# q and k times their inverse length as one VectorE instruction, and the inverse key sums as 128 rows of 16 columns

## The chip, the cores and the metric

The kernel runs on one core of one Trainium2 chip. The engines are PE (TensorE), DVE (VectorE), ACT (ScalarE) and POOL (GpSimd); SP issues most of the DMAs. The metric is the device time of one launch in microseconds. All arithmetic that the change touches is float32.

## The reference

x has 32 sequences of 256 positions of 256 channels. A recurrent layer (a projection to 512 channels, a causal convolution of four taps, a normalisation, a scan over the 256 positions with 16 states and a gate) gives the input of two attention layers, each followed by a gated feed-forward. x is added to the end result. What the change touches is in the attention layer:

```python
l2norm = lambda t: t / jnp.clip(jnp.linalg.norm(t, axis=-1, keepdims=True), 1e-12)
q, k = l2norm(q) * qs, l2norm(k) * ksc          # 8 heads of 64
q, k = rotary_xpos(q, k)
sim = jnp.where(mask, -max, einsum('bhwid,bhwjd->bhwij', 8 * q, k))   # windows of 128
attn = softmax(sim, axis=-1)
out = einsum('bhwij,bhwjd->bhwid', attn, v)
x = x + out @ wo
```

Two inverses are in it: that of the length of each head's q and k, limited from below, and that of the sum of the exponentials of each query.

## The kernel before

The 32 sequences go in four groups of eight. The scan of a group takes 256 steps, eight sequences at once: at each step SP loads a row of xn, spread over 128 partitions (`load_rows`, L685, six steps ahead), ACT scales it by beta (`scale_row`, L706), DVE takes the step (`step`, L716, one custom instruction of 128x512, whose inputs h and xrep lie in SBUF), and PE reads the states out (`read_out`, L728). Every 32 steps (a chunk) come the convolution of the next chunk (xr L472, acc L478 on POOL and L489 on DVE, xc L509), its normalisation (statistics on DVE, the power -1/2 on POOL in L565, L572 and L579 on ACT), the decays (bcd L632, ad L648, pd L650, pi L653, beta L654), the sum of skip and readout (xd L779) and the gate (zT L799, read by PE in L808).

While group g is scanned, group g-1 goes through attention and feed-forward: 64 pairs of sequence and layer in all. Each pair is a sequence of stages, eight stages (`ST = 8`) to a pair and about two scan steps to a stage; the pairs overlap. `attend` and `feed` (L1458 and L1479) put the functions into numbered stages: `stage(n, i, what)` is stage 8n + i. Two pairs take one chunk of 32 scan steps. The convolution and the decays of a chunk fall into the second of the two, which is called odd here, the other even.

In a pair, for each of two windows w: PE projects v, q and k (`project_qkv`, L989, into PSUM banks of 128x512). For q and k `rotated` (L998) follows: ACT squares (sq, L1002), DVE multiplies by the cosine and sine tables (rot L1005, swp L1010 twice), POOL adds the two (L1013), DVE sums the squares by head (L1015) and limits the sum from below by 1e-24 (L1019), POOL takes the power -1/2 (rn, L1021), and POOL multiplies the rotated tile by it (L1022). `turn` (L1025) transposes the result with PE (L1028), and ACT copies it. Then come the scores on PE (L1215), the exponentials on ACT (L1227) and the masks (L1238 on POOL, L1243 on DVE). `sums` (L1246) adds the exponentials with PE (L1252), into rows of a bank: 16 equal rows for each of the eight heads, 256 columns; DVE takes the reciprocal of all 128x256 (rinv, L1260). `values` (L1263) multiplies with v (L1271), and ACT copies to oT (L1278). `put_inverse` (L1281) stores one of each 16 rows to a tensor in DRAM, `load_inverse` (L1285) reads it back, each head's row spread over 64 partitions (rb), `divide` (L1293) multiplies oT by it on DVE, and `finish` projects (ps_wo, L1039) and adds to the residual (res, L1047). In the feed-forward `widen` (L1361) projects into pa (L1375), ACT applies the Gelu to one half (ag, L1386), DVE multiplies by the other (`product`, L1393), and `narrow` (L1398) projects back (po_f, L1402) and adds (fo or res, L1413).

The PSUM banks are eight and are handed round among all of these, so a projection waits for whoever read the bank's former content. A scheduler orders each engine's instructions at build time, by the order of the program and by when it takes their inputs to be ready; `tc.keep_in_program_order` pins an instruction behind all that its engine was given before. On the chip each engine takes its list strictly in order and waits at an instruction until its inputs are there; so does SP with its DMAs.

Of the kernel before, what the change touches and what calls it, by code (L numbers as in the profile page):

```python
# [10 lines left out]
FP = mybir.dt.float32  # L11
BF = mybir.dt.bfloat16
I32 = mybir.dt.int32
AF = mybir.ActivationFunctionType
ALU = mybir.AluOpType
# [4 lines left out]
P = 128  # L20
S = 256
# [15 lines left out]
HEADS = 8  # L37
DH = 64
W = 128
NW = S // W  # L40
# [12 lines left out]
def bc(ap, axis, n):  # L53

    ap = ap.unsqueeze(axis)
    shape = list(ap.shape)
    shape[axis] = n
    return ap.broadcast_to(shape)
# [15 lines left out]
def kernel(  # L74
# [29 lines left out]
    nc = tc.nc  # L104
# [4 lines left out]
    const = ctx.enter_context(tc.tile_pool(name="const", bufs=1))  # L109
# [14 lines left out]
    with tc.tile_pool(name="setup", bufs=1) as setup:  # L124
        sq = setup.tile([1, L, 2, DH], FP, tag="sq", name="sq")
# [37 lines left out]
    for j in range(NJ):  # L163
# [5 lines left out]
    nc.gpsimd.memset(one, 1.0)  # L169
    neg_half = const.tile([P, HEADS], FP, tag="neg_half", name="neg_half")  # L170
    nc.gpsimd.memset(neg_half, -0.5)
    half = const.tile([P, NJ], FP, tag="half", name="half")
    nc.gpsimd.memset(half, 0.5)

# [7 lines left out]
        out=mask_t[:, 0:W], in_=mask_t[:, 0:W], compare_op=ALU.is_ge, fill=MASKED_LOW,  # L182
# [3 lines left out]
        out=mask_t[:, W : 2 * W], in_=mask_t[:, W : 2 * W], compare_op=ALU.is_ge,  # L186
# [11 lines left out]
    rs_sb = const.tile([P, L, NW, 2, DH], FP, tag="rs_sb", name="rs_sb")  # L198
# [18 lines left out]
    for i in range(2):  # L217
        t = const.tile([P, NI * (P + GB)], FP, tag=f"ly{i}", name=f"ly{i}")
# [3 lines left out]
    def program(ctx, exact):  # L222
# [6 lines left out]
        dp = ctx.enter_context(tc.tile_pool(name="dp", bufs=3, space=DRAM))  # L229
        ap_ = ctx.enter_context(tc.tile_pool(name="at", bufs=2, reuse_waits="tile"))  # L230
        aw = ctx.enter_context(tc.tile_pool(name="aw", bufs=3, reuse_waits="tile"))
        ps_w = ctx.enter_context(tc.tile_pool(name="psw", bufs=8, space=PSUM, reuse_waits="tile"))

        def bank(pool, tag, name):
            return pool.tile([P, DI], FP, tag=tag, name=name)
# [748 lines left out]
        def project_qkv(b, w, a):  # L984
            ps = bank(ps_w, "w", "ps_qkv")
            for k in range(KM):

                t0 = 1 - k + w * W
                nc.tensor.matmul(  # L989
                    ps,  # L990
                    res[b][:, k, t0 : t0 + W],
                    wt["qkv", a][:, k],
                    start=(k == 0),
                    stop=(k == KM - 1),
                )
            return ps

        def rotated(l, ps, w, a):  # L998


            sq = ap_.tile([P, DI], FP, tag="swp", name="sq", bufs=3)
            nc.scalar.activation(sq, ps, AF.Square)  # L1002
            rot = ap_.tile([P, HEADS, DH], FP, tag="rot", name="rot", bufs=4)
            ph = ps.rearrange("p (h d) -> p h d", h=HEADS)
            nc.vector.tensor_mul(rot, ph, bc(rc_sb[:, l, w, a], 1, HEADS))  # L1005
            swp = ap_.tile([P, HEADS, DH], FP, tag="swp", name="swp", bufs=3)
            hd = DH // 2
            for i in range(2):
                o, s = slice(i * hd, (i + 1) * hd), slice((1 - i) * hd, (2 - i) * hd)
                nc.vector.tensor_mul(  # L1010
                    swp[:, :, o], ph[:, :, s], bc(rs_sb[:, l, w, a, o], 1, HEADS)
                )
            nc.gpsimd.tensor_add(rot, rot, swp)  # L1013
            ss = aw.tile([P, HEADS], FP, tag="ss", name="ss")
            nc.vector.tensor_reduce(  # L1015
                ss, sq.rearrange("p (h d) -> p h d", h=HEADS), AX.X, ALU.add
            )

            nc.vector.tensor_scalar_max(ss, ss, 1e-24)  # L1019
            rn = aw.tile([P, HEADS], FP, tag="rn", name="rn")  # L1020
            nc.gpsimd.tensor_tensor(rn, ss, neg_half, ALU.pow)  # L1021
            nc.gpsimd.tensor_mul(rot, rot, bc(rn, 2, DH))  # L1022
            return rot

        def turn(rot, dst):  # L1025
            tr = ps_w.tile([P, HEADS // 2, W], FP, tag="w", name="tr_qk")
            for hp_ in range(HEADS // 2):
                nc.tensor.transpose(  # L1028
                    tr[:, hp_, :],
                    rot[:, 2 * hp_ : 2 * hp_ + 2, :].rearrange("p h d -> p (h d)"),  # L1030
                    ident,
                )
            nc.scalar.copy(dst, tr)
# [15 lines left out]
        if exact:  # L1049
# [4 lines left out]
                out=mask[:, 0:W], in_=mask[:, 0:W], compare_op=ALU.is_ge, fill=MASKED,  # L1054
# [3 lines left out]
                out=mask[:, W : 2 * W], in_=mask[:, W : 2 * W], compare_op=ALU.is_ge, fill=MASKED,  # L1058
# [3 lines left out]
        def attention(l):  # L1062

            for b in range(GB):

                qTs, kTs, vs = [], [], []
                for w in range(NW):
                    for a in (2, 0, 1):
                        ps = project_qkv(b, w, a)
                        if a == 2:  # L1070
                            v_sb = ap_.tile([P, DI], FP, tag="v1", name="v_sb", bufs=3)
                            nc.scalar.copy(v_sb, ps)
                            vs.append(v_sb)
                            continue
                        rot = rotated(l, ps, w, a)
                        dst = ap_.tile(
                            [P, HEADS // 2, W], FP, tag="kT1" if a else "qT1",
                            name="kT" if a else "qT", bufs=3 if a else 2,
                        )
                        turn(rot, dst)  # L1080
                        (kTs if a else qTs).append(dst)
                        yield

                oT = ap_.tile([P, NC_, S], FP, tag="oT", name="oT", bufs=1)
                for w in range(NW):
# [6 lines left out]
                    for h0 in range(0, HEADS // 2, nh):  # L1092
                        for r in range(2):
# [21 lines left out]
                            for i, h in enumerate(hs):  # L1115
                                nc.scalar.activation(
                                    p_sb[:, i, :], p_sb[:, i, :], AF.Exp,
                                    bias=nmax[:, h : h + 1],
# [19 lines left out]
                    rinv = aw.tile([P, HEADS], FP, tag="rinv", name="rinv")  # L1138
# [15 lines left out]
        class Attention:  # L1154
# [9 lines left out]
            def project(self, b, w, a):  # L1164
# [8 lines left out]
                else:  # L1173
                    self.rot[b, w, a] = rotated(self.l, ps, w, a)

            def turn(self, b, w):
                for a in range(2):
                    turn(
                        self.rot.pop((b, w, a)), self.qkv[b][a][:, :, w * W : (w + 1) * W]
                    )  # L1180
# [65 lines left out]
            def sums(self, b):  # L1246

                rs = bank(ps_w, "w", "rs")[:, 0:S]
                for kw in range(NW):
                    for r in range(2):  # L1250
                        for i in range(HEADS // 2):
                            nc.tensor.matmul(  # L1252
                                rs[32 * i : 32 * i + 32, kw * W :],
                                head_cols[:, r],
                                self.p[b, kw, i, r],
                                start=(kw == 0 and r == 0),
                                stop=(kw == NW - 1 and r == 1),
                            )
                rinv = aw.tile([P, S], FP, tag="rinv", name="rinv", bufs=1)
                nc.vector.reciprocal(rinv, rs)  # L1260
                self.rinv = rinv

            def values(self, b):  # L1263
                oT = ap_.tile([P, NC_, S], FP, tag="oT", name="oT", bufs=1)
# [13 lines left out]
                    nc.scalar.copy(oT[:, i0 : i0 + 2], ov)  # L1278
                self.o[b] = oT

            def put_inverse(self):  # L1281
                self.inv = dp.tile([HEADS, S], FP, tag="inv", name="inv")
                nc.sync.dma_start(out=self.inv, in_=self.rinv[0 : P : P // HEADS])

            def load_inverse(self):  # L1285

# [168 lines left out]
        def stage(n, i, what, *args):  # L1455
            stages.setdefault(ST * n + i, []).append(partial(what, *args))

        def attend(n, at, b, nxt):  # L1458

            stage(n, 0, at.turn, b, 1)  # L1460
            stage(n, 2, at.scores, b, (0, 0, 2), (1, 0, HEADS // 2))
            stage(n, 3, at.scores, b, (0, 2, 2))
            stage(n, 3, at.mask, 1, 0)
            if at.apart:
                for i, what in ((3, (0, 0)), (4, (0, 2))):
                    stage(n, i, at.mask, *what)
            stage(n, 7, at.sums, b)
            stage(n, 7, at.values, b)
            stage(n + 1, 0, at.put_inverse)
            stage(n + 1, 2, at.load_inverse)  # L1470
            stage(n + 1, 4, at.divide, b)
            stage(n + 1, 6, at.finish, b)
            if nxt is not None:
                for w in range(NW):
                    for i, a in ((0, 2), (1, 0), (1, 1)):
                        stage(n, 3 * w + i, nxt[0].project, nxt[1], w, a)
                stage(n, 6, nxt[0].turn, nxt[1], 0)

        def feed(n, g, l, b):  # L1479
# [23 lines left out]
        ats = [Attention(g, l) for g, l, _ in seqs]  # L1503

        for n, (g, l, b) in enumerate(seqs):
            nxt = (ats[n + 1], seqs[n + 1][2]) if n + 1 < len(seqs) else None
# [7 lines left out]
        def scan_to(s):  # L1514
            while done[0] is None or done[0] < s:
                done[0] = next(scan, 1 << 30)
# [9 lines left out]
        for w in range(NW):  # L1526
            for a in (2, 0, 1):
                ats[0].project(0, w, a)
                scan_to(done[0] + 1)
        ats[0].turn(0, 0)  # L1530
        s0 = done[0]
        group, reload = ST * L * GB, ST * (L * GB - GB + 6) + 2
# [129 lines left out]
```

## Time and profile before

| | us |
|---|---|
| three runs | 3581.7, 3597.07, 3590.51 (median 3590.51) |
| the profiled execution | 3582.75 |
| its span | 3581.0 |
| mean granted clock of PE | 0.992 of full speed |
| DVE busy in the span's first 500 us / 500 to 2800 / after | 413 / 1852 / 402 |
| PE busy in the same stretches | 446 / 2226 / 773 |

Attention begins at about 475 us; the last scan step starts at 2796 us. A row of groups reads: line, engine, operation, tiles written and read, shapes, count, then busy time in us, mean ns of one, and after the second bar the idle time of the engine ahead of it with what ended it. A row of waits reads: who waited, for whom, us in total, times, longest us. A row of a timeline reads: start, duration, engine, line, operation, tiles, and in brackets the idle time before it and what ended it.

### The profile page before, as it was taken

What the parts mean: (1) busy time and instruction counts of PE and PEld (TensorE: products, weight loads), DVE (VectorE), ACT (ScalarE), POOL (GpSimd) and SP (SyncE); (2) the same over time, 40 slices, a digit from 0 to 9 for tenths busy, and PEclk for the clock granted to TensorE, in tenths of its full rate; (3) what the DMA queues carried; (4) which work ended last, traced back from release to release, by engine and by line L of the source; (5) the groups of instructions that cost most, each with busy time, mean ns of one, the idle gap of its engine ahead of it and who ended that gap; (6) DMA issues with size and microseconds to landing.
All of it is one profiled execution on the core that took longest, in us unless ns stands there. A gap on an engine that the chain in (4) does not pass through costs nothing.

```text
span 3581.0 us, 57673 instructions
## 1 busy us (share of the span) xinstructions
PE 3446.0 (96%) x20220; PEld 2253.9 (63%) x20220; DVE 2667.3 (74%) x5049; ACT 1998.7 (56%) x3599; POOL 1892.2 (53%) x1842
## 2 busy tenths in 40 slices
PE   7999989999999999999999999999999999999999
PEld 4555335666656666666666666666666677777777
DVE  5888889888788777888787778888877555555553
ACT  4666656656555665566566655655666444434442
POOL 4433477645556555655565556555544454544551
PEclk9999999999999999999999999999999999999999
DMA  7887665445354545444454555534454112011101
GB/s 207 219 221 213 198 174 149 120 117 143 109 144 125 149 141 148 130 118 127 118 142 125 138 149 140 143 106 131 114 141 122 54 50 61 13 30 38 33 27 37
DMA packets 468767, 435.68 MB, mean 122 GB/s; under 512 B 228723, under 2 KB 308084, under 8 KB 468340
## 3 DMA queue, kind: packets, MB, share of 16 engines
q1 hardware_dynamic: 384018, 419.88, 42.0%
q10 hardware_dynamic: 84450, 12.01, 2.0%
q8 instruction: 163, 2.67, 0.3%
q14 instruction: 136, 1.11, 0.1%
HBM read 383.54 MB, written 46.66 MB: 120 GB/s over the span
## 4 chain that ended last, share of the span: by engine, by line
PE 61%; DVE 19%; DMA 7%; POOL 6%; ACT 4%; issue 3%; SPq 0%; ACTq 0%; DVEq 0%; POOLq 0%
PE ps_qkv L989 13%; PE pa L1375 13%; DVE h L716 7%; PE po_f L1402 7%; DMA xrep<-xnd 5%; PE ps_wo L1039 5%; PE y L728 4%; PE ov L1271 4%; PE sc L1215 3%; PE ps_out L808 3%; PE ps_in L399 2%; PE tr_qk L1028 2%; PE rs L1252 2%; ACT xrep L706 2%; DVE acc L489 2%
## 5 line engine op out<-in xcount | busy, mean ns | idle before, releaser
L716 DVE CUSTOM_DVE_ANT_0 h<-h,xrep,lim 128x512 f32<-128x512 f32 x1024 | 961.0, 938 | 228.9 <-ACT xrep L706 196.6
L706 ACT ACTIVATE xrep<-xrep,beta 128x512 f32<-128x512 f32 x960 | 672.3, 718 | 341.4 <-DMA xrep<-xnd 219.8
L989 PE MATMUL ps_qkv<-qkv,res 128*128 128x512 f32 x1536 | 713.5, 601 | 17.9 <-DVE rinv L1260 8.4
L1375 PE MATMUL pa<-hT,w 128*128 128x256 f32 (+1 forms) x2816 | 675.1, 382 | 11.3 <-DVE zT L799 10.7
L1375 PEld LDWEIGHTS pa<-hT,w 128*128 128x128 f32 (+1 forms) x2816 | 516.9, 188 | 152.9 <-issue 35.4
L1013 POOL TENSOR_TENSOR rot<-rot,swp 128x512 f32<-128x512 f32 x256 | 339.9, 1328 | 475.3 <-DVE swp L1010 423.5
L1021 POOL TENSOR_TENSOR rn<-ss,neg_half 128x8 f32<-128x8 f32 x256 | 466.8, 1823 | 18.4 <-DVE ss L1019 7.8
L989 PEld LDWEIGHTS ps_qkv<-qkv,res 128*128 128x128 f32 x1536 | 282.2, 191 | 301.6 <-issue 241.4
L728 PE MATMUL y<-h,ly 128*32 128x512 f32 x2048 | 348.9, 609 | 16.9 <-DVE h L716 13.9
L1327 POOL TENSOR_TENSOR rstd<-ve,neg_half 128x2 f32<-128x2 f32 x64 | 46.9, 733 | 527.6 <-DVE ve L1325 511.3
L1393 DVE SCALAR_TENSOR_TENSOR ag<-pa,b_sb,ag 128x256 f32<-128x256 f32 x320 | 151.6, 474 | 222.4 <-ACT ag L1386 222.3
L1402 PE MATMUL po_f<-ag,w 128*128 128x256 f32 x1280 | 309.0, 389 | 5.9 <-DVE fo L1413 3.8
L1022 POOL TENSOR_TENSOR rot<-rot,rn 128x512 f32<-128x512 f32 x256 | 289.4, 1130 | 20.0
L1402 PEld LDWEIGHTS po_f<-ag,w 128*128 128x128 f32 x1280 | 236.8, 191 | 71.3 <-issue 12.0
L1386 ACT ACTIVATE ag<-pa,b_sb 128x256 f32<-128x256 f32 x320 | 150.2, 469 | 233.1 <-PE pa L1375 232.1
L1002 ACT ACTIVATE sq<-ps_qkv 128x512 f32<-128x512 f32 x256 | 150.8, 595 | 185.1 <-PE ps_qkv L989 119.4
L1039 PE MATMUL ps_wo<-oT,wo 128*128 128x256 f32 x1024 | 231.7, 379 | 0.5 <-DVE ag L1393 0.5
L489 DVE SCALAR_TENSOR_TENSOR acc<-xr,wc_sb,acc 128x256 f32<-128x256 f32 x384 | 195.1, 531 | 47.7 <-POOL acc L478 47.2
L1005 DVE TENSOR_TENSOR rot<-ps_qkv,rc_sb 128x512 f32<-128x512 f32 x256 | 174.8, 683 | 65.6 <-ACT sq L1002 65.0
L1039 PEld LDWEIGHTS ps_wo<-oT,wo 128*128 128x128 f32 x1024 | 194.4, 190 | 28.1 <-DVE ag L1393 0.9
L1227 ACT ACTIVATE pT<-sc 128x512 f32<-128x512 f32 x384 | 202.3, 603 | 7.6 <-PE sc L1215 5.8
L1271 PE MATMUL ov<-pT,v_sb 128*64 128x256 f32 (+1 forms) x2048 | 183.7, 330 | 19.4 <-DVE ag L1393 19.3
(160 smaller groups left out, 5482.8 us busy)
## 6 DMA issues: line engine op xcount, KB each, us to landing
xrep<-xnd SPq DMA_DIRECT2D x960, 256.0 KB
rb<-inv SPq DMA_DIRECT2D x128, 256.0 KB
xnd<-xn SPq DMA_DIRECT2D x64, 256.0 KB
qkv<-in_wqkv_dram SPq DMA_DIRECT2D x24, 512.0 KB
ahead<-xs_a SPq DMA_DIRECT2D x48, 256.0 KB
xp<-ahead SPq DMA_DIRECT2D x48, 256.0 KB
xd<-xnd SPq DMA_DIRECT2D x192, 64.0 KB
w<-in_w_dram SPq DMA_DIRECT2D x80, 128.0 KB
```

What stands on the lines that cost most here:

```text
L489: nc.vector.scalar_tensor_tensor(acc, xr[:, :, k : k + CH], wc_sb[:, ch, k : k + 1], acc, ALU.mult, ALU.add,)
L706: scaled = nc.scalar.activation(bx, ck[c].pop(("bx", t), bx), AF.Copy, scale=ck[c]["beta"][:, t : t + 1])
L716: nc.vector._custom_dve(TENSOR_ADD_SAT, out=h_new, in0=state["h"], in1=bx, s0=ck[c]["lim"][:, 0, t : t + 1], s1=ck[c]["lim"][:, 1, t : t + 1],
L728: nc.tensor.matmul(ck[c]["y", hb][32 * q : 32 * q + 32, :], ly[hb % 2][:, 32 * t : 32 * t + 32], ck[c].pop(("h", hb * TB + t)), start=(i = ...
L989: nc.tensor.matmul(ps, res[b][:, k, t0 : t0 + W], wt["qkv", a][:, k], start=(k == 0), stop=(k == KM - 1),)
L1013: nc.gpsimd.tensor_add(rot, rot, swp)
L1021: nc.gpsimd.tensor_tensor(rn, ss, neg_half, ALU.pow)
L1022: nc.gpsimd.tensor_mul(rot, rot, bc(rn, 2, DH))
L1039: nc.tensor.matmul(po[:, d], wt["wo", 0][:, c, d * P : (d + 1) * P], oT[:, c, :], start=(c == 0), stop=(c == NC_ - 1),)
L1271: nc.tensor.matmul(ov[r * DH : (r + 1) * DH, i, kw * W :], self.qkv[b][2][:, kw, h * DH : (h + 1) * DH], self.p.pop((b, kw, i0 + i, r)), s ...
L1375: nc.tensor.matmul(dst[x], wt["w1", m][:, k, x], self.h[:, k], start=(k == 0), stop=(k == KM - 1),)
L1402: nc.tensor.matmul(self.po[:, d], wt["w2", 0][:, m, d * P : (d + 1) * P], self.ag[m], start=(m == 0), stop=(m == len(MCH) - 1),)
```

## The change

The limit and the product with the inverse length become one scalar_tensor_tensor on DVE, min(rn, 1e12) times rot, in a function `unit` of its own. It is pinned, and `normed` puts it two stages after the projection of q and k. The squares get a bias of 2e-19 (tile `tiny`) ahead of squaring. The sums of the exponentials are copied from PSUM by ACT, one of each 16 rows is stored to DRAM, read back as 128 rows of 16 columns, inverted there by DVE (pinned), stored to DRAM, and read back spread as before. The divide moves from stage 4 to stage 5.

```diff
+    tiny = const.tile([P, 1], FP, tag="tiny", name="tiny")
+    nc.gpsimd.memset(tiny, 2e-19)
...
-            nc.scalar.activation(sq, ps, AF.Square)
+            nc.scalar.activation(sq, ps, AF.Square, bias=tiny)
...
-
-            nc.vector.tensor_scalar_max(ss, ss, 1e-24)
             rn = aw.tile([P, HEADS], FP, tag="rn", name="rn")
             nc.gpsimd.tensor_tensor(rn, ss, neg_half, ALU.pow)
-            nc.gpsimd.tensor_mul(rot, rot, bc(rn, 2, DH))
+            return rot, rn
+
+        def unit(rot, rn):
+
+            tc.keep_in_program_order(
+                nc.vector.scalar_tensor_tensor(
+                    rot, bc(rn, 2, DH), 1e12, rot, ALU.min, ALU.mult
+                )
+            )
             return rot
...
+            def normed(self, b, w):
+                for a in range(2):
+                    self.rot[b, w, a] = unit(*self.rot[b, w, a])
...
-                rinv = aw.tile([P, S], FP, tag="rinv", name="rinv", bufs=1)
-                nc.vector.reciprocal(rinv, rs)
-                self.rinv = rinv
+                self.rs = aw.tile([P, S], FP, tag="rinv", name="rs_sb", bufs=1)
+                nc.scalar.copy(self.rs, rs)
...
+            def put_sums(self):
+                self.sm = dp.tile([HEADS, S], FP, tag="sums", name="sums")
+                nc.sync.dma_start(out=self.sm, in_=self.rs[0 : P : P // HEADS])
+
+            def load_sums(self):
+                self.r16 = aw.tile([P, HEADS * S // P], FP, tag="r16", name="r16", bufs=1)
+                nc.sync.dma_start(
+                    out=self.r16,
+                    in_=self.sm.rearrange("h (q t) -> (h q) t", q=P // HEADS),
+                )
+
+            def invert(self):
+                tc.keep_in_program_order(nc.vector.reciprocal(self.r16, self.r16))
+
             def put_inverse(self):
                 self.inv = dp.tile([HEADS, S], FP, tag="inv", name="inv")
-                nc.sync.dma_start(out=self.inv, in_=self.rinv[0 : P : P // HEADS])
+                nc.sync.dma_start(
+                    out=self.inv.rearrange("h (q t) -> (h q) t", q=P // HEADS), in_=self.r16
+                )
...
-            stage(n + 1, 0, at.put_inverse)
-            stage(n + 1, 2, at.load_inverse)
-            stage(n + 1, 4, at.divide, b)
+            stage(n + 1, 0, at.put_sums)
+            stage(n + 1, 1, at.load_sums)
+            stage(n + 1, 2, at.invert)
+            stage(n + 1, 2, at.put_inverse)
+            stage(n + 1, 3, at.load_inverse)
+            stage(n + 1, 5, at.divide, b)
             stage(n + 1, 6, at.finish, b)
             if nxt is not None:
                 for w in range(NW):
                     for i, a in ((0, 2), (1, 0), (1, 1)):
                         stage(n, 3 * w + i, nxt[0].project, nxt[1], w, a)
+                    stage(n, 3 * w + 3, nxt[0].normed, nxt[1], w)
                 stage(n, 6, nxt[0].turn, nxt[1], 0)
...
+        for w in range(NW):
+            ats[0].normed(0, w)
         ats[0].turn(0, 0)
```

The path for large scales (not taken with these inputs) calls `unit(*rotated(...))` at once.

## The prediction

> **What bounds the kernel now.** First the page's busy times, then the waits of PE between 500 and 2800 us (there the scan and the attention of another group run side by side), then the timelines of PE and DVE over one period.
>
> ```profile
> PE 3446.0 (96%) x20220; PEld 2253.9 (63%) x20220; DVE 2667.3 (74%) x5049; ACT 1998.7 (56%) x3599; POOL 1892.2 (53%) x1842
> PE 61%; DVE 19%; DMA 7%; POOL 6%; ACT 4%; issue 3%; SPq 0%; ACTq 0%; DVEq 0%; POOLq 0%
> ```
>
> PE is busy for 96% of the span and leads the chain that ended last. The change touches no matmul, so it can only win where PE stands still. Who makes it stand still, in total us, times and longest:
>
> ```profile
> PE ov L1271 <- DVE ag L1393: 19.3, 14, 1.5
> PE pa L1375 <- DVE zT L799: 10.7, 8, 1.9
> PE ps_qkv L989 <- DVE rinv L1260: 8.4, 14, 0.9
> ...
> PE ps_qkv L989 <- DVE xd L779: 2.6, 9, 0.5
> ```
>
> These four, 41.0 us or 1.1% of the span, are all waits for DVE, and they come back in every period of 32 scan steps (103 us, two sequences of attention). From 2800 us on PE waits for DVE 0.6 us in all; before 500 us its waits are for loads and the scan. One period, from the start of one wait to the end of the third:
>
> ```profile
> 1977.39 1.99 PE L1375 MATMUL pa<-hT,w 128*128 128x256 f32 x8 [1.16 <-DVE zT L799]
> ...
> 1983.64 1.52 PE L1271 MATMUL ov<-pT,v_sb 128*64 128x256 f32 x16 [1.37 <-DVE ag L1393]
> ...
> 1990.16 1.98 PE L989 MATMUL ps_qkv<-qkv,res 128*128 128x512 f32 x4 [0.78 <-DVE rinv L1260]
> ```
>
> ```profile
> 1975.73 1.01 DVE L1019 TENSOR_SCALAR ss<-ss 128x8 f32<-128x8 f32 x1
> 1976.66 0.68 DVE L799 TENSOR_TENSOR zT<-tz,sg 128x512 f32<-128x512 f32 x1
> ...
> 1980.16 1.02 DVE L648 TENSOR_SCALAR ad<-ad,a_sb 128x32 f32<-128x32 f32 x1
> 1981.10 1.83 DVE L716 CUSTOM_DVE_ANT_0 h<-h,xrep,lim 128x512 f32<-128x512 f32 x1
> ...
> 1983.04 0.45 DVE L1393 SCALAR_TENSOR_TENSOR ag<-pa,b_sb,ag 128x256 f32<-128x256 f32 x1
> ...
> 1988.36 1.75 DVE L1260 RECIPROCAL rinv<-rs 128x256 f32<-128x256 f32 x1
> ```
>
> DVE has no idle time from 1962.9 to 1986.2 us: in this odd sequence of the period it is late, and PE waits three times. A limit over 8 columns (L1019) takes 1.01 us right ahead of zT, though the fastest of its kind takes 0.15; POOL was running its product L1022 then (1975.55, 1.17 us). The ad of 32 columns, 1.02 us, ran beside the next L1022 (1980.08, 1.07 us). In the even sequence (1990 to 2043 us) DVE has idle times of 2.84 and 5.79 us, and PE waits only 0.52 us, for xd.
>
> **The change, part by part.** Rows (count, busy us, mean ns):
>
> ```profile
> L716 DVE CUSTOM_DVE_ANT_0 h<-h,xrep,lim 128x512 f32<-128x512 f32 x1024 | 961.0, 938 | 228.9 <-ACT xrep L706 196.6 <-DVE h L716 8.7 <-PE y L728 2.3
> L1022 POOL TENSOR_TENSOR rot<-rot,rn 128x512 f32<-128x512 f32 x256 | 289.4, 1130 | 20.0
> L1019 DVE TENSOR_SCALAR ss<-ss 128x8 f32<-128x8 f32 x256 | 119.8, 468 | 0.6
> L1260 DVE RECIPROCAL rinv<-rs 128x256 f32<-128x256 f32 x64 | 112.0, 1750 | 11.1 <-PE rs L1252 10.6 <-DMA rw<-raw 0.5
> L1295 DVE TENSOR_TENSOR oT<-oT,rb 128x1024 f32<-128x1024 f32 x64 | 77.6, 1213 | 0.0
> ```
>
> POOL loses 256 products, 289.4 us. POOL is not the bound, but its next work comes 2.2 us earlier per pair of q and k (two products).
>
> DVE loses 256 limits (119.8 us) and 64 wide reciprocals (112.0 us). It gains 256 products of 128x512 with two inputs from SBUF. No row has this form. A scalar_tensor_tensor of 256 columns takes 478 ns (L1413); from 256 to 512 columns L1010 (415) and L1005 (683) grow by 268; so 0.75 us, 192 us in all. The ends are half of L1295, 0.61 (156 us), and the scan step L716 with its two SBUF inputs, 0.94 (241 us). The narrow reciprocal: 1750 ns at 256 columns, 341 at 32 (L653), so 6.3 ns a column and 0.24 us at 16, 15 us in all. DVE's sum is 192 + 15 - 120 - 112 = -25 us (-61 to +24). As a total that matters little; its place does.
>
> ACT gains 64 copies of 128x256 from PSUM, between 0.36 (64x256, L526) and 0.58 (128x512, L1278); I take 0.45, 29 us, beside PE. It stands ahead of the copies of oT and delays them by that; ps_wo, which needs them, runs some 35 us later. The bias of the square adds no instruction.
>
> SP gets two more small DMAs per sequence. One put and the wait for its landing took 1.72 us (inv issued at 1990.14, rb behind it at 1991.86). So the sums go out behind the copy at about 1988.5, are back after two trips at 1992.0, and the built order has the reciprocal just ahead of the next q (before: 1998.8): 6.8 us of cover. Behind it on DVE wait the q and k work and the scan steps, should this cover go. On SP the put of the inverse now waits for that DVE reciprocal; the loads of xrep behind it need a later scan step anyway. The divide stands one stage later and, by the even sequence's times (done at 2019.8, ps_wo at 2023.4), still 3.6 us ahead of ps_wo.
>
> Now the odd sequence by the built order. (1) Two products (1.5 us) come in front of the convolution, at 1956.3. There DVE waited 0.47, 0.30 and 0.64 us for POOL's acc (L478), which comes 2.2 us sooner: net +0.1; the reordered block behind it (xc, acc, xr, divide) keeps its sum, and some 0.9 us of small gaps and long xc go; DVE reaches q about 1.0 us sooner at best, 0 at worst. (2) Two L1019 go, 0.34 and 1.01 us: zT is 1.3 to 2.3 us sooner, and PE's 1.16 us **goes**. (3) Then ag: res (0.67 us) and two products (1.5) now stand ahead of it; against that the 1.3 to 2.3 won, and up to 1.0 each in ad and in the h of 1.83 us. So ag comes about 1 us earlier than before, and PE, no longer held at zT, arrives 1.16 earlier: this wait **stays**. (4) rs leaves PSUM by the ACT copy at about 1988.3 instead of 1990.1: PE's 0.78 **goes**, and the bank's next user is not late. (5) In the even sequence L1019 (0.33 + 0.16) leaves the queue ahead of xd and 0.24 enters: 0.3 of 0.5 us of that wait goes.
>
> Sum over the span: zT 10.7 + rinv 8.4 + xd 1.6 = **20.7 us** less. The profiled execution took 3582.75 us (span 3581.0), which gives 3562. The median of the runs shown is 3590.51, 7.8 above it; a median of new runs is then 3569.8, my number.
>
> A rule against this change: the row h L716 takes 0.81 us in its median, 0.94 in its mean, and 1.83 beside POOL's xd (1981.11, 1.27 us). [...]
>
> **Rivals.**
> A, the product runs at 0.94 us because POOL is at work beside it: four of them ahead of ag, 4 x 0.19 = 0.76 us later in each of 22 periods, 17 us: the gain shrinks to 4 us, 3586. For: h's mean. Against: part of h's excess came from the L1022 that goes.
> B, ag's wait goes too, since ad and h lose their POOL neighbour and (1) gives its full 1.0 us: 41 us less, 3549. Against: POOL's xd still stands there.
> C, slower: the even sequence becomes like the odd one. The divide (1.2 us) leaves DVE's idle time at 2015 us and stands behind ag at 2018.5, ahead of q and k; with the two products behind them (1.5) DVE is up to 2.7 us later where PE now never waits. It decides if PE's slack there is under that. If PE loses 2 us in each of 22 even sequences, the sum is +44 - 21 = +23, 3614. Against: zT was done at 2023.5 and first used at 2027.7, 4.2 us of slack, and the idle time of 5.79 us behind takes up the products. For: PSUM banks freed by ag and q have a slack that no row shows.
> D, the narrow inverse lands late and holds DVE. It needs 6.8 us more than the row; I give it little. From 0 at that point each us costs up to 64.
>
> **How the numbers follow.** Forecast 0.44, A 0.28, B 0.10, C 0.14, D 0.04. About 0.5% (18 us) is what a measurement here can tell from no change, so faster means under 3572.6. The forecast lies just beyond: a sixth of its 0.44 falls within. Faster 0.37 + 0.10 and a little of A: 0.50; slower C and D less 0.03 that stays within, 0.15; the same 0.35. The range takes in B (less 10 for PE waits on h and fo that also shrink) and the product's upper end with half of C: 3539 to 3601.
>
> **What would show it.** Right: no PE wait on rinv's successor and none on zT, ag still the first of PE's waits; product at 0.7 to 0.8 us; ad's median (1015 ns) lower; DVE some 25 us less, POOL 289 less; DVE never waiting at the narrow reciprocal. Wrong: products near 1 us, a new PE wait between 2005 and 2043 us of the like period, or DVE idle in front of the reciprocal.

## The result and the profile after

The changed kernel takes 3546.99 us (median of 4 runs, 3541.36 to 3553.66), the kernel before 3589.3 (4 runs, 3581.7 to 3597.07). The ratio is 0.9883, 95% interval 0.9865 to 0.9902: 42 us faster. The forecast was 21. The profiled execution took 3553.66 us, with a span of 3551.9.

First the page's busy times and the shares of the chain that ended last, in the changed kernel:

```profile
PE 3441.7 (97%) x20220; PEld 2263.7 (64%) x20220; DVE 2605.5 (73%) x5049; ACT 2037.4 (57%) x3663; POOL 1620.7 (46%) x1587
PE 64%; DVE 16%; DMA 7%; ACT 5%; POOL 4%; issue 3%; SPq 1%; ACTq 0%; DVEq 0%; POOLq 0%
```

PE's work is the same, its share grew, and DVE's share of the chain fell from 19 to 16%. DVE lost 62 us of busy time, POOL 272, and ACT gained 39. Where PE stood still is best seen in the stretches 1000 to 2500 us, here their sum lines, before and after:

```profile
sum 1500.00, PE 1453.63 PEld 963.51 DVE 1205.73 ACT 899.74 POOL 878.06; mean PE 484.54 PEld 321.17 DVE 401.91 ACT 299.91 POOL 292.69
```

```profile
sum 1500.00, PE 1480.16 PEld 982.25 DVE 1190.16 ACT 937.99 POOL 773.47; mean PE 493.39 PEld 327.42 DVE 396.72 ACT 312.66 POOL 257.82
```

PE's idle time there went from 46.4 to 19.8 us. This number (1500 less PE's busy time) is used below for every kernel. One period of 32 scan steps took 102.3 us before and 99.6 after (mean over steps 448 to 896, by the starts of h). The stretch from the last scan step to the end is 785.2 us before and 785.3 after. From the first scan step to the last it is 2748.3 and 2707.4 us, 40.8 less; the two spans differ by 29.1 only since in this one execution the scan began 11.7 us later (at 59.2): the granted clock was 0.63 from 20 to 40 us and 0.67 from 40 to 60, against 1.00 and 0.83 before. Of the 40.8 us, 24.6 are idle time of PE; the other 16.2 stand in the profile as shorter busy time of the same matmuls, whose ends are modelled. An estimate from the granted clock (0.997 against 0.989 over 586 us of PE work in steps 448 to 640) puts some 5 of them down to it; the rest is open.

Who makes PE wait between 500 and 2800 us, in the changed kernel (total us, times, longest):

```profile
PE ps_wo L1047 <- DVE oT L1322: 11.2, 4, 6.1
PE ps_qkv L991 <- DVE ag L1420: 7.2, 12, 1.4
...
PE pa L1402 <- DVE zT L801: 5.1, 7, 0.7
PE ps_qkv L991 <- DVE xd L781: 4.5, 13, 0.4
```

The wait of ov on ag, 19.3 us and first of all before, is not in the list any more. That of ps_qkv on the reciprocal (8.4) is gone too, zT's is halved (10.7), xd's grew (2.6). The odd sequence that the prediction walked through, on PE and then on DVE:

```profile
1961.11 2.00 PE L1402 MATMUL pa<-hT,w 128*128 128x256 f32 x8 [0.68 <-DVE zT L801]
...
1964.47 2.82 PE L1282 MATMUL ov<-pT,v_sb 128*64 128x256 f32 x32
```

```profile
1955.59 0.68 DVE L1007 TENSOR_TENSOR rot<-ps_qkv,rc_sb 128x512 f32<-128x512 f32 x1
...
1960.37 0.68 DVE L801 TENSOR_TENSOR zT<-tz,sg 128x512 f32<-128x512 f32 x1
...
1963.80 1.26 DVE L650 TENSOR_SCALAR ad<-ad,a_sb 128x32 f32<-128x32 f32 x1
...
1965.69 0.68 DVE L1055 TENSOR_TENSOR res<-res,ps_wo 128x512 f32<-128x512 f32 x1
1966.29 1.28 DVE L1027 SCALAR_TENSOR_TENSOR rot<-rn,rot 128x512 f32<-128x512 f32 x2
...
1967.69 0.45 DVE L1420 SCALAR_TENSOR_TENSOR ag<-pa,b_sb,ag 128x256 f32<-128x256 f32 x1
```

Measured from the first rot of this sequence, zT starts at 4.78 us (5.71 before) and this ag at 12.10 (12.09 before). So ag is exactly as late as it was, and yet PE runs all 32 ov matmuls (1964.47 to 1967.29) without a stop, before this ag has even begun. The forecast cannot explain this, and the experiments start from it.

The rows of the parts:

```profile
L718 DVE CUSTOM_DVE_ANT_0 h<-h,xrep,lim 128x512 f32<-128x512 f32 x1024 | 931.9, 910 | 215.1 <-ACT xrep L708 166.5 <-PE y L730 21.4 <-DVE h L718 8.9
L1027 DVE SCALAR_TENSOR_TENSOR rot<-rn,rot 128x512 f32<-128x512 f32 x256 | 196.1, 804 | 5.0 <-POOL rn L1021 4.7
L1304 DVE RECIPROCAL r<-r 128x16 f32<-128x16 f32 x64 | 15.0, 235 | 0.0
```

```profile
L1004 ACT ACTIVATE sq<-ps_qkv,tiny 128x512 f32<-128x512 f32 x256 | 172.4, 685 | 172.2 <-PE ps_qkv L991 143.8 <-DMA out_dram<-fo 14.3 <-POOL xr L473 4.7
...
L1272 ACT COPY rs_sb<-rs 128x256 f32<-128x256 f32 x64 | 23.3, 364 | 35.1 <-PE rs L1264 33.0 <-DMA xs<-in_xT_dram 1.0 <-DMA xrep<-xnd 1.0
```

### The profile page after: what moved, and what is told of

Its sections match the earlier page's. It is cut to its first block, busy times and chain, and to the rows that moved or that the text cites. A ratio compares the mean times of both kernels' runs of the same rounds, so it can differ in the third digit from the quotient of the medians.

```text
span 3551.9 us, 57690 instructions
## 1 busy us (share of the span) xinstructions
PE 3441.7 (97%) x20220; PEld 2263.7 (64%) x20220; DVE 2605.5 (73%) x5049; ACT 2037.4 (57%) x3663; POOL 1620.7 (46%) x1587
## 3 DMA queue, kind: packets, MB, share of 16 engines
q14 instruction: 137, 1.12, 0.1%
## 4 chain that ended last, share of the span: by engine, by line
PE 64%; DVE 16%; DMA 7%; ACT 5%; POOL 4%; issue 3%; SPq 1%; ACTq 0%; DVEq 0%; POOLq 0%
PE ps_qkv L991 13%; PE pa L1402 13%; PE po_f L1429 6%; DVE h L718 6%; DMA xrep<-xnd 5%; PE y L730 5%; PE ps_wo L1047 5%; PE ov L1282 4%; PE ps_in L401 3%; PE ps_out L810 3%; PE sc L1227 3%; PE tr_qk L1036 2%; PE rs L1264 2%; ACT xrep L708 2%; DVE acc L491 2%
## 5 line engine op out<-in xcount | busy, mean ns | idle before, releaser
L718 DVE CUSTOM_DVE_ANT_0 h<-h,xrep,lim 128x512 f32<-128x512 f32 x1024 | 931.9, 910 | 215.1 <-ACT xrep L708 166.5
L1015 POOL TENSOR_TENSOR rot<-rot,swp 128x512 f32<-128x512 f32 x256 | 349.0, 1363 | 543.7 <-DVE swp L1012 513.0
L730 PE MATMUL y<-h,ly 128*32 128x512 f32 x2048 | 335.8, 606 | 9.8 <-DVE h L718 9.2
L1429 PEld LDWEIGHTS po_f<-ag,w 128*128 128x128 f32 x1280 | 235.3, 190 | 64.8 <-DVE xc L511 11.7
L1004 ACT ACTIVATE sq<-ps_qkv,tiny 128x512 f32<-128x512 f32 x256 | 172.4, 685 | 172.2 <-PE ps_qkv L991 143.8
L1047 PE MATMUL ps_wo<-oT,wo 128*128 128x256 f32 x1024 | 236.2, 385 | 14.2 <-DVE oT L1322 11.2
L491 DVE SCALAR_TENSOR_TENSOR acc<-xr,wc_sb,acc 128x256 f32<-128x256 f32 x384 | 188.6, 523 | 46.4 <-POOL acc L480 45.9
L1012 DVE TENSOR_TENSOR swp<-ps_qkv,rs_sb 128x256 f32<-128x256 f32 x512 | 191.8, 416 | 29.8 <-POOL rot L1015 29.6
L1027 DVE SCALAR_TENSOR_TENSOR rot<-rn,rot 128x512 f32<-128x512 f32 x256 | 196.1, 804 | 5.0 <-POOL rn L1021 4.7
```

Source lines behind the costliest of these rows:

```text
L491: nc.vector.scalar_tensor_tensor(acc, xr[:, :, k : k + CH], wc_sb[:, ch, k : k + 1], acc, ALU.mult, ALU.add,)
L718: nc.vector._custom_dve(TENSOR_ADD_SAT, out=h_new, in0=state["h"], in1=bx, s0=ck[c]["lim"][:, 0, t : t + 1], s1=ck[c]["lim"][:, 1, t : t + 1],
L730: nc.tensor.matmul(ck[c]["y", hb][32 * q : 32 * q + 32, :], ly[hb % 2][:, 32 * t : 32 * t + 32], ck[c].pop(("h", hb * TB + t)), start=(i = ...
L1027: nc.vector.scalar_tensor_tensor(rot, bc(rn, 2, DH), 1e12, rot, ALU.min, ALU.mult)
L1047: nc.tensor.matmul(po[:, d], wt["wo", 0][:, c, d * P : (d + 1) * P], oT[:, c, :], start=(c == 0), stop=(c == NC_ - 1),)
L1429: nc.tensor.matmul(self.po[:, d], wt["w2", 0][:, m, d * P : (d + 1) * P], self.ag[m], start=(m == 0), stop=(m == len(MCH) - 1),)
```

## The experiments

Theory 1: the gain comes from VectorE's lead, and the limit L1019 is its main loss. Theory 2: it comes from the wide reciprocal and the PSUM bank that it holds. All runs were timed in five rounds against the kernel before. The table gathers them; "idle" is PE's idle time from 1000 to 2500 us, "ag" the start of the middle ag of the odd sequence, in us behind its first rot. Both are of one execution and one stretch, so they follow the ratio only roughly: e_nobias_divide4, say, has 33.0 us of idle time here against 19.8 in the changed kernel, but 18.3 against 30.5 from 500 to 1000 us.

| kernel | ratio, 95% interval | idle | ag |
|---|---|---|---|
| before | 1 | 46.4 | 12.1 |
| changed | 0.9883 (0.9865 to 0.9902) | 19.8 | 12.1 |
| e_product | 0.9921 (0.9907 to 0.9934) | 30.7 | 10.3 |
| e_sums | 0.9995 (0.9983 to 1.0006) | 52.3 | 12.7 |
| e_limit_only | 0.9904 (0.9889 to 0.9919) | 25.5 | 9.2 |
| e_wide_copy | 0.9907 (0.9892 to 0.9922) | 28.0 | 12.1 |
| e_limit_sums | 0.9902 (0.9882 to 0.9921) | 30.8 | 9.8 |
| e_limit_kept | 0.9927 (0.9907 to 0.9946) | 37.3 | 12.4 |
| e_after_nobias | 0.9971 (0.9957 to 0.9985) | 44.8 | 13.1 |
| e_divide4 | 0.9889 (0.9867 to 0.9912) | 33.5 | 10.3 |
| e_limit_reduce | 0.9884 (0.9867 to 0.9900) | 28.6 | 9.3 |
| e_limit_pool | 0.9968 (0.9955 to 0.9980) | 41.5 | 9.2 |
| e_nobias_divide4 | 0.9865 (0.9850 to 0.9880) | 33.0 | 10.3 |
| e_reduce_sums | 0.9881 (0.9863 to 0.9900) | 27.4 | 9.3 |

### Each part alone

The product part: the changed kernel with the old `sums`, `put_inverse` and stages.

```diff
-                self.rs = aw.tile([P, S], FP, tag="rinv", name="rs_sb", bufs=1)
-                nc.scalar.copy(self.rs, rs)
+                rinv = aw.tile([P, S], FP, tag="rinv", name="rinv", bufs=1)
+                nc.vector.reciprocal(rinv, rs)
```

> The product on VectorE alone, with the limit in it; the inverse key sums as before (a reciprocal of 256 columns read from PSUM). Theory 1, VectorE's lead: the waits for zT and ag go because two limits and the GpSimd product beside them left the odd sequence, so this part brings 25 to 32 us of the 42 (3557 to 3564, with before at 3589), and the wait on rinv (8.4 us) stays. Theory 2, the wide reciprocal: it is the 1.75 us at the end of the sequence, with the bank that it holds, that make the next sequence late; then this part brings at most 12 us (3577 or more) and the wait on ag stays above 10 us.

0.9921, 28 us: theory 1. Here the build puts ag ahead of the products, and ov waits 4.0 us in all.

The sums part: the kernel before with the new `sums`, the two more DMAs, the narrow reciprocal and its stages.

```diff
-                rinv = aw.tile([P, S], FP, tag="rinv", name="rinv", bufs=1)
-                nc.vector.reciprocal(rinv, rs)
+                self.rs = aw.tile([P, S], FP, tag="rinv", name="rs_sb", bufs=1)
+                nc.scalar.copy(self.rs, rs)
```

> The key sums alone: ScalarE's copy out of PSUM, two more small DMAs, a reciprocal of 16 columns; limit and GpSimd product as before. Theory 1: only the waits on rinv and part of xd go, 10 us (3579), and the waits on zT and ag stay at 8 to 11 and 15 to 20 us. Theory 2: 25 us or more (3564 or less), with ag's wait under 8 us. If the two parts add, this run and the product alone sum to 42 us.

Nothing (0.9995), against both theories. The wait on the reciprocal is gone, and so is that of ov on ag; others took their place:

```profile
PE ps_qkv L989 <- DVE ag L1408: 12.2, 14, 1.7
PE ps_qkv L989 <- ACT oT L1277: 10.8, 13, 1.6
PE pa L1390 <- DVE zT L799: 10.5, 9, 1.9
PE ov L1270 <- ACT xn L579: 8.6, 14, 1.2
```

So two waits of 27.7 us went, and the time did not move. All waits of PE in this stretch sum to 81.2 us, against 72.4 before: while VectorE's odd sequence is late, PE stops at one tile or another. The parts don't add either: 28 and 2 us alone, 42 together.

The limit alone: the product stays on GpSimd.

```diff
-            nc.scalar.activation(sq, ps, AF.Square)
+            nc.scalar.activation(sq, ps, AF.Square, bias=tiny)
...
-            nc.vector.tensor_scalar_max(ss, ss, 1e-24)
```

> Only the limit goes (its instruction of 8 columns on VectorE; the squares get the small bias); the product stays on GpSimd, the sums as before. VectorE loses 120 us of busy time. Theory 1, with the limit as its main part: zT's wait goes (10 us) and ag's shrinks to under 10, 15 to 25 us in all (3564 to 3574). If instead the product's leaving GpSimd is what counts (less contention in the scan step, in ad and in xd), the gain is under 8 us (above 3581).

0.9904, 34 us: more than the whole product part. PE's waits, from the same view:

```profile
PE ps_qkv L991 <- DVE rinv L1261: 5.8, 9, 0.9
...
PE ps_qkv L991 <- DVE ag L1394: 3.6, 7, 0.9
...
PE pa L1376 <- DVE zT L801: 1.9, 7, 0.4
```

VectorE's order is that of the kernel before, less the limits. ag starts 2.9 us earlier behind rot: 1.35 us are the two limits, 0.8 the ad behind them (0.23 in place of 1.02), 1.0 the h after it (0.81 in place of 1.83), less small gaps:

```profile
1971.52 0.23 DVE L650 TENSOR_SCALAR ad<-ad,a_sb 128x32 f32<-128x32 f32 x1
1971.77 0.81 DVE L718 CUSTOM_DVE_ANT_0 h<-h,xrep,lim 128x512 f32<-128x512 f32 x1
```

With that zT's wait falls to 1.9 us in all, and ov no longer waits for ag.

The changed kernel with the wide reciprocal, taken from ScalarE's copy:

```diff
-                tc.keep_in_program_order(nc.vector.reciprocal(self.r16, self.r16))
+                tc.keep_in_program_order(nc.vector.reciprocal(self.rs, self.rs))
```

> The changed kernel, but with the reciprocal of all 256 columns taken on VectorE from ScalarE's copy, so without the two more DMAs: the PSUM bank is free as early as in the changed kernel, VectorE has 1.5 us more work in each of 64 sequences. If the early bank is the sums part's whole worth: 3547, the same as the changed kernel. If it is VectorE's 1.5 us at the end of the odd sequence: in 22 periods up to 33 us at worst, and, as only the odd sequences are late, rather 8 to 15 us slower than the changed kernel (3555 to 3562).

0.9907, about 9 us behind the changed kernel, within the 8 to 15 expected of VectorE's 1.5 us per sequence; the intervals of the two overlap. PE has a wait here that the changed kernel lacks, for VectorE's swp (10.4 us, 10 times).

### What the limit waits for

The kernel e_limit_only with the same edit as e_sums:

> Limit gone (small bias on the squares) and the key sums as in the changed kernel; the product stays on GpSimd. So far the limit alone gave 0.9904, the product with its limit 0.9921, the sums alone 0.9995, both parts 0.9883. If the sums pay wherever the odd sequence has lost the limit, their 14 us come here too: 0.986 to 0.988, as fast as the changed kernel or faster, and the move of the product to VectorE is worth nothing. If the sums pay only with the product on VectorE (which takes work from GpSimd), this stays at 0.990 to 0.991.

0.9902: with the limit gone and the product on GpSimd the sums bring nothing. Next the changed kernel with the limit kept:

```diff
+            nc.vector.tensor_scalar_max(ss, ss, 1e-24)
             rn = aw.tile([P, HEADS], FP, tag="rn", name="rn")
```

> The changed kernel, with the limit instruction of 8 columns kept on VectorE (256 of them). Theory, the limit is the main part since it stands in VectorE's queue right ahead of zT: 20 to 34 us of the 42 are lost (0.993 to 0.998). Rival, what made it dear was the GpSimd product that ran beside it (1.01 us against 0.15): without that product it costs 0.15 to 0.2 each, 40 to 50 us of VectorE in all, and under 10 us of the time (below 0.991).

0.9927: some 16 us are lost, between theory and rival. The limit did not become cheap without its neighbour, it found another one: its mean rose to 606 ns, since GpSimd now runs the addition L1015 beside it. The one ahead of zT in an odd sequence took 1.24 us, from 1868.83 to 1870.07, and that addition ran from 1868.53 to 1870.04. So it is not the product alone that makes it dear: the addition, another GpSimd instruction of 512 columns, does the same. To separate "it is there" from "it waits for GpSimd", the kernel before got the limit in the same place and number, in another form:

```diff
-                ss, sq.rearrange("p (h d) -> p h d", h=HEADS), AX.X, ALU.add
+                pair[:, :, 0], sq.rearrange("p (h d) -> p h d", h=HEADS), AX.X, ALU.add
...
-            nc.vector.tensor_scalar_max(ss, ss, 1e-24)
+            nc.vector.tensor_reduce(ss, pair, AX.X, ALU.max)
```

> The kernel before, with the limit in its place and number, but written as a reduction by maximum over pairs (the sum beside a constant 1e-24) in place of the instruction with a scalar; PSUM banks as before. Theory, lock: the limit of before takes 0.13 us by itself and up to 1.25 us because it waits for the GpSimd instruction that is running; the reductions of the traces never grew beside GpSimd (668 to 676 ns at 512 columns), so this limit takes 0.15 to 0.25 us always, two of them in the odd sequence cost 0.4 instead of 1.35 us, and most of the gain of taking the limit out comes: 0.991 to 0.994 (22 to 32 us). Rival, its mere place in the queue and its being there: within 0.3% of the kernel before (0.997 or more).

0.9884: with this one instruction written otherwise the kernel is as fast as with the whole change, within the intervals. The limit's duration (ns, shortest, median and longest) in the kernel before, in e_limit_kept and in e_limit_reduce:

```profile
L1019 DVE TENSOR_SCALAR ss<-ss x256: 152/334/1249, 478.0 to 3491.4; 128x8 f32<-128x8 f32 x128
```

```profile
L1020 DVE TENSOR_SCALAR ss<-ss x256: 131/342/1261, 483.9 to 3481.2; 128x8 f32<-128x8 f32 x128
```

```profile
L1024 DVE TENSOR_REDUCE ss<-pairs x256: 147/159/170, 483.6 to 3473.1; 128x8 f32<-128x16 f32 x128
```

In these three runs the form with a scalar took 0.13 us at the least and 1.26 at the most, the reduction never more than 0.17. In the kernel before, the limit and the ad of the prediction's timeline end (at 1976.74 and 1981.18) when GpSimd's products do:

```profile
1975.55 1.17 POOL L1022 TENSOR_TENSOR rot<-rot,rn 128x512 f32<-128x512 f32 x1
...
1980.08 1.07 POOL L1022 TENSOR_TENSOR rot<-rot,rn 128x512 f32<-128x512 f32 x1
```

1975.55 + 1.17 = 1976.72 and 1980.08 + 1.07 = 1981.15: in both cases the small instruction was done 0.02 to 0.03 us after GpSimd's. Over the whole trace, 188 limits started while a GpSimd instruction of 512 columns was running; 182 of them took over 250 ns, and every one of these ended within 0.06 us of it. The 41 that started ahead of the GpSimd instruction beside them took 162 ns in the mean. What makes the form with a scalar wait and the reduction not, a lock or something else, no run shows.

The limit on GpSimd, ahead of the power:

```diff
-            nc.vector.tensor_scalar_max(ss, ss, 1e-24)
+            nc.gpsimd.tensor_scalar_max(ss, ss, 1e-24)
```

> The kernel before, with the limit of 8 columns on GpSimd, ahead of the power there; nothing is left out. VectorE loses 256 instructions (120 us), GpSimd gains 256 small ones. If the limit on VectorE was the loss, as with the limit taken out (0.9904): 0.990 to 0.992. If GpSimd's later power and product now hold the transposes of q and k: a wait of PE on the product, and 0.994 or more.

0.9968, 11 us only, though VectorE's odd sequence is that of e_limit_only (zT at 4.79, ag at 9.24). GpSimd's chain for q and k is longer by 396 ns each, and the convolution behind it comes later:

```profile
1963.96 0.48 DVE L489 SCALAR_TENSOR_TENSOR acc<-xr,wc_sb,acc 128x256 f32<-128x256 f32 x1 [1.08 <-POOL acc L478]
```

In the same place of e_limit_only this wait is 0.47 us, and over 1500 to 2500 us VectorE waits for GpSimd's acc 19.6 us in place of 13.5. That is 6.1 us in ten periods; the two kernels differ by 23 us in 22 periods, some 1 us in each. So it accounts for over half, and the rest is open.

### Order and bank

The changed kernel without the bias:

```diff
-            nc.scalar.activation(sq, ps, AF.Square, bias=tiny)
+            nc.scalar.activation(sq, ps, AF.Square)
```

> The changed kernel without the small bias on the squares (leaves out the offset of 2e-19). A square goes back from 685 to 595 ns, 22 us less of ScalarE, and VectorE's rot, which comes behind the square, starts 0.09 earlier. If the lead of VectorE at the odd sequence's start is what still counts: 2 to 6 us faster than the changed kernel (0.9865 to 0.988). If ScalarE's time is hidden: the same within 2 us.

0.9971, far outside both expectations: with less work the kernel loses 31 of its 42 us. Its first wait of PE:

```profile
PE ps_wo L1047 <- DVE oT L1322: 45.7, 15, 4.1
```

In the changed kernel the division stands ahead of q and k in the odd sequence (1954.46, rot at 1955.59). Without the bias the build takes q to be ready sooner and puts q and k first, the division 4.1 us behind the first rot; PE reaches ps_wo 2.5 us behind rot and waits 2.9 us. The test of that reading moves the division back to its old stage:

```diff
-            stage(n + 1, 5, at.divide, b)
+            stage(n + 1, 4, at.divide, b)
```

> The changed kernel without the small bias on the squares (leaves out the offset of 2e-19), and with the division one stage earlier. The same without the bias alone lost 31 of the 42 us, with 45.7 us of PE waiting for the division, which the build had put behind q and k in the odd sequence. If that place is the whole reason: the division stands ahead of q and k again, PE waits for it less than 10 us in all, and the ratio is 0.986 to 0.990. If the bias itself matters in another way: 0.994 or more, with no wait for the division.

0.9865, and no wait of PE on the division in the list: its place was the reason. Not all of the loss was waiting: from scan step 640 to 896 the kernel without the bias was granted a clock of 0.980, the changed kernel 1.000, and PE was busy 12.7 us longer there, beside 15.9 us more idle time. Over whole runs the clock was 0.981 to 0.986 in its 12 runs, 0.986 to 0.991 in the changed kernel's and 0.990 to 0.994 here, so that the clock came back with the division's place. This is the best ratio of all, though its interval overlaps the changed kernel's.

The same move of the division, in the changed kernel with its bias:

> The changed kernel with the division one stage earlier, where it stood before. The build puts the second ov tile of the odd sequence again on the PSUM bank that pa held and ag frees (in the changed kernel it has a bank that the copy of qT frees). If that choice of bank is why the wait of ov on ag went: ag still ends 12.5 us behind rot, the second ov tile could start 10.3 behind it, so PE waits some 2 us in each of 22 odd sequences, the wait is back at 25 to 45 us in all, and the kernel is 15 to 40 us slower than the changed one (0.993 to 0.999). If the wait went since VectorE is early enough: the same as the changed kernel within 5 us, no wait of ov on ag above 5 us in all.

0.9889, as the changed kernel, and ov waits for ag 2.9 us in all. The run did not test the bank by itself, as it was meant to: in this build ag too stands earlier again, ahead of res and the products (10.3). But it shows the pair. The banks of the second ov tile in an odd sequence, by the built programs, and the order of the three around ag:

| build | VectorE's order | last content of ov's bank |
|---|---|---|
| before, e_limit_only | ag, res | pa, freed by ag |
| e_product, e_divide4 | ag, res, product, product | pa, freed by ag |
| e_sums | res, ag | tr_qk, freed by the copy of qT |
| changed, e_wide_copy | res, product, product, ag | tr_qk, freed by the copy of qT |

Whenever one of these builds puts ag behind res, it also gives ov another bank, and the one that ag frees goes to a tile of PE three places later. Had ov kept that bank in the changed kernel, its second tile, due about 10.3 us behind rot, would have waited until 12.5. An experiment with that bank alone was not made, so its 2.2 us are worked out and not measured.

Last, e_limit_reduce with the edit of e_sums, the division at its old stage:

> The limit as a reduction over pairs (0.9884 by itself), and the key sums of the changed kernel, with the division kept at its old stage; the product stays on GpSimd. In this build the PSUM banks of the odd sequence are those of the kernel before. If the sums were worth nothing alone only because their build changed the banks and put the residual addition ahead of ag, then here the wait on rinv (6.4 us) goes with nothing in its place: 0.985 to 0.987. If the sums are worth nothing in any build: 0.988 to 0.990, with waits of ps_qkv on oT or ag in place of rinv.

0.9881 against 0.9884 for the reduction alone: the wait on the reciprocal is gone, and this came in its place:

```profile
PE ps_qkv L994 <- DVE ag L1413: 8.5, 11, 0.9
PE ps_qkv L994 <- DVE xd L784: 5.6, 13, 0.6
```

## Why the prediction was half right

The sign and the place were right: PE is the bound, and the gain comes mainly from PE's waits for VectorE between the first and the last scan step. It had 21 us where 42 were measured. That 42 is near the 41 of its rival B is luck: B wanted ag to come early enough, which it does in e_limit_only and e_limit_reduce (9.2 and 9.3) and not here. It is luck, too, that all waits of PE from 500 to 2800 us fell by 20.6 us (72.4 to 51.8), the forecast's sum: of its four waits 31.4 us went, and other waits grew by 10.8.

- **Step (3), ag's wait stays: wrong, and this is the main error.** The order was right, res and two products ahead of ag. It put ag about 1 us earlier; behind rot it did not move (12.09 to 12.10), since res and the products took what zT, ad and h gave. By the prediction's own terms PE should then have waited longer. It does not wait at all (19.3 us to none), because of the bank: the step took the order of the changed build and the banks of the old one, and the same build that put ag back took it out of ov's way. In size those 19.3 us are near the gap of 21, but what the bank is worth in time no run shows: e_sums lost the same wait and won nothing, and e_limit_reduce, with the old bank, is as fast as the changed kernel.
- **Step (1), VectorE reaches q 0 to 1.0 us sooner: wrong.** From the fo ahead of the convolution to the first rot it takes 15.5 us (1940.13 to 1955.59), against 15.0 before (1955.95 to 1970.95). VectorE's three waits for acc were to be gone, as GpSimd lost its product; they are 0.46, 0.30 and 0.39 us, after 0.47, 0.30 and 0.64. GpSimd did come free sooner, but then it stood idle until VectorE's xc, which now comes behind the two products:

```profile
1942.25 1.43 POOL L480 TENSOR_SCALAR acc<-xr,wc_sb,bconv_sb 128x256 f32<-128x256 f32 x2 [2.68 <-DVE xc L511]
```

- **Step (2), two limits go: right in kind, and undervalued.** zT came 0.93 us earlier behind rot, and its wait was halved to 5.1, not gone; 0.26 us of the gain went to a new wait of VectorE for GpSimd's addition. But taking the limit out brings 34 us alone, by the limit itself, ad and h together, and keeping it in the changed kernel costs some 16. The prediction saw all three beside GpSimd and named "up to 1.0 each in ad and in the h", and then priced only zT's wait and 1.6 us at xd. In the changed kernel ad still stands beside xd (1.26): its median fell only from 1015 to 926 ns, and its mean rose from 710 to 762.
- **Step (4), rinv's wait goes: right as a wait (8.4 to none), wrong as a gain.** Alone, and with the limit out of the way, the sums part is worth 0 to 2 us. Behind the product it is worth some 14 (0.9921 to 0.9883), about 9 of them by the narrow reciprocal. A likely reason is that VectorE has the products to do there; no run shows it.
- **Step (5), xd: wrong.** It grew from 2.6 to 4.5.
- **Sizes.** Product 0.75 expected, 0.80 in the mean and 196.1 us in all, 192 expected; narrow reciprocal 0.235 for 0.24, with no wait ahead of it; ScalarE's copy 0.364 for 0.45. VectorE's sum is -62 us instead of -25, for h lost 29 (961.0 to 931.9), xc 8 and acc 6.5. xc is shorter in every build with the product on VectorE and in no other; h fell as far in e_limit_reduce, which keeps the product on GpSimd, so that its loss is not the product's alone. Missed: the bias of the square adds no instruction but 90 ns to each, 595 to 685, 22 us of ScalarE.
- **Rival A, the product longer beside GpSimd.** Right for single instructions: 154 of the 256 products ran clear of GpSimd's instructions of 512 columns, at 0.68 us in the mean, 102 beside one, at 0.99 and up to 1.77. In the odd sequence they ran clear (1.28 for two), so PE does not see it. The limit grew beside GpSimd as well (167 ns in the mean alone, up to 1249), and there the form that does not grow was worth as much as the whole change; the prediction counted such growth only against the change.
- **Rival C, the division behind q and k.** It shows in the first sequences, up to 1152 us (PE waits 11.2 us, 4 times), and in 13 odd sequences of e_after_nobias, against one of the changed kernel. 90 ns of a square decided it.
- **Rival D.** No run showed VectorE waiting long for the narrow inverse: 0.0 us in the row of the changed kernel, 2.7 in e_reduce_sums, the most. The next q, which the prediction put at 1998.8, started at 1999.29 in the kernel before; the cover was 0.5 us longer than it said.

## What to carry to other kernels

A tiny instruction in the queue of a busy engine is priced by what it waits for: here a limit over 8 columns took 0.17 us alone and up to 1.25 beside a GpSimd instruction of 512 columns, and written as a reduction never over 0.17. So ask of a small VectorE instruction which GpSimd instruction runs beside it in the trace, and try another form of the same arithmetic. Where a scheduler and a pool of PSUM banks make the program, read order and banks of the changed build together before saying that a wait stays or goes, and expect that a change of 90 ns can turn the order, as in e_after_nobias, which kept 11 of the 42 us. A wait that goes is only worth what the next late tile leaves: two waits of 27.7 us went in e_sums, and nothing was won.

## What the runs showed of the hardware

- The limit in the kernel before, a VectorE instruction with a scalar over 8 columns in SBUF, took 167 ns in the mean where no GpSimd instruction of 512 columns overlapped it (27 of 256). Started while one ran, it took up to 1249 and ended with it (182 of 188); started first, it took 162. The reduction over 16 columns in e_limit_reduce took 147 to 170 in all 256 cases, 203 of them started while such an instruction ran. The sum of squares (L1015, a reduction of 512 columns) took 662 to 679 in all 256 of the kernel before, 129 of them beside one, though only 4 started while it ran.
- Of the other VectorE instructions of the kernel before, acc and h, whose inputs lie in SBUF, grew: acc took 0.49 us in the mean alone and 1.16 beside a GpSimd instruction of 512 columns, h 0.81 and 1.12. The means of rot, swp, zT and xd, which read PSUM, differ by under 10 ns. The division, with both inputs in SBUF, took 1.21 in all 64 cases; it was never the second to start.
- ScalarE's square of 128x512 from PSUM takes 595 ns, and 685 with its bias from a tile in SBUF.
- In the profiled execution of the kernel before, the 5049 instructions of VectorE, 3409 activations and copies of ScalarE, 1842 instructions of GpSimd and 1914 DMAs of SP run in the order of the built lists, without an exception. In e_after_nobias PE stood 2.90 us before a ps_wo, for the division, and ran nothing that its list has behind it until then.
